# Row sums, block ends and embedding products of an attention layer at other places in TensorE's order

## The chip, the cores and the metric

The kernel runs on one core of a Trainium2 chip. Its engines work side by side, each through its own queue in order: TensorE (PE in the profile, its weight loads PEld), VectorE (DVE), ScalarE (ACT), GpSimd (POOL) and SyncE (SP), which here issues most of the DMA transfers. TensorE writes its results into PSUM banks; the others read them there. The metric is the device time of one execution in microseconds (us). The kernel before takes 2664.66 us, the median of three runs (2664.56 to 2665.32).

## The reference

Two layers on `x` of 2 x 512 x 64 x 32, so two images of 2048 tokens with 512 channels, all in float32. Only the first layer is touched by the change:

```python
q = concat(x, emb) @ Wq          # emb: 64 channels, made of row and column
k = concat(x, emb) @ Wk
v = x @ Wv
attn = softmax(q @ k.T / sqrt(64))        # 8 heads, 2048 x 2048 each
x = attn @ v @ Wout + bout + x
```

After it each token is normalized over its channels, and the second layer follows: a landmark attention with an iterated pseudo-inverse and a short convolution, and a feed-forward step whose two matrices the kernel multiplies into one (the "feed-forward map") while the first layer runs. The map is made of four-bit codes by compare and add on VectorE.

## The kernel before

The first layer is done as eight attentions, one for each image and pair of heads (two heads of 64 channels fill the 128 partitions): four of image 0, then four of image 1. `attention0` (L1263) does one of them. It has four query blocks `t` of 512 tokens, and for each 16 steps `c` of 128 keys: 64 steps, taken two at a time. One pass of its loop, two steps, is called a **round** here (round 0 to 31, and a last one, 32, without scores). A round does, in this order in the program:

- `scores` of its two steps: TensorE multiplies in the 64x64 form (L1275), ScalarE takes the exponential from PSUM to SBUF (L1283). There are two buffers for scores and six for exponentials.
- `add`: VectorE adds the exponentials into the running row sums of the block (L1293).
- `values` of the two steps of the round before: TensorE multiplies in the 64x64 form (L1305). At the last step of a block ScalarE copies one of the two result banks (L1311) and VectorE adds the other (L1312). There is one buffer for each of the two banks, so that the next block's first values wait for these two.
- a **burst**, where the round's number stands in `BURSTS`: a piece of other work on TensorE, mostly in the 128x128 form, taken from a generator up to its next `REST`.
- after a block's end the row sums: `sums_of` adds over the partitions with TensorE (L799), VectorE takes the reciprocal (L1320), eight transfers spread it (L810), GpSimd multiplies (L1323).
- in a round without a burst one call from the list `soon`, or, if that is empty and the round stands in `TABLE`, one step of the feed-forward map (L1359 to L1375).

The end of a block falls into rounds 8, 16 and 24, and that of the last block into round 32, before the next attention begins.

The bursts of an attention compute the next one's inputs (`Heads0.units`, L1065): for a pair of heads the embedding's part (`few`, L955, one small product for q and one for k, from which GpSimd or VectorE makes blocks `e`, L974), q and k in two halves (`products`, L1014, seven products each in a scheme of Strassen's kind, whose token differences VectorE makes at L911 by calls in `soon`), then the values (L1143), beside which steps of the feed-forward map run. Their end finds the largest |q| and |k| (L1126). The fifth attention's bursts also project, add and normalize image 0 (`finish0_units`: L1158 and L1165, then `statistics`, with a reciprocal at L1215). Banks of the projections, sums and normalization share two PSUM buffers (`bank`).

Each engine's order is the program's order; there is no planner. Lines below are the profile's.

Of the kernel before, what the change touches and what calls it, by code (L numbers as in the profile page):

```python
# [10 lines left out]
F32 = mybir.dt.float32  # L11
I32 = mybir.dt.int32
AF = mybir.ActivationFunctionType
# [3 lines left out]
P = 128  # L17
# [20 lines left out]
def general_path(  # L38
# [632 lines left out]
GAP = object()  # L671
REST = object()

TABLE = 9, 10, 11, 12, 16, 17, 18, 19, 20, 21, 22, 25, 27
NVS = 3, 3, 3, 1
FEW = (2, 1), (1, 2), (1, 1), (2, 2)
BURSTS = (
    *[(1, 6, 14, 23)] * 3, (4, 10, 17, 25), (1, 3, 6, 9, 11, 14, 17, 19, 22, 25, 27, 30),
    (4, 12, 21), (4, 12, 21), (12, 22),
)  # L680


# [1 line left out]
def fast_path(  # L684
# [99 lines left out]
    eps = const.tile([P, 1], F32, name="eps1")  # L784
    nc.vector.memset(eps, 1e-5)
    b0_sb = const.tile([P, KC], F32, name="b0_f")
    bound = const.tile([P, 3 * B * NPAIR], F32, name="bound1")
    zs = const.tile([P, 2], F32, name="zs1")
    rsum = const.tile([P, B * NPAIR, 4], F32, name="rsum1")
# [136 lines left out]
    class Heads0:  # L926
# [22 lines left out]
        def queries(self):  # L949
            self.q = qopool.tile([P, S], F32, tag="qo", name=f"q_{self.name}")  # L950

        def few(self, kind):

            fp = bank(f"fp_{kind}_{self.name}")
            nc.tensor.matmul(fp[:, : H + W], lhsT=self.w[kind][1], rhs=emb_sb, start=True, stop=True)  # L955
            ft = self.ft[kind] = wpool0.tile([P, H + W], F32, tag=f"ft{kind}", name=f"ft_{kind}_{self.name}")
            nc.vector.tensor_copy(ft, fp[:, : H + W])

        def embed(self, n=1):

# [105 lines left out]
        def units(self, xbs, parts, after=None, ready=None):  # L1066

            self.xbs = xbs
            self.begin()
            values = self.values()  # L1070
            if self.b == 0:
                for kind in "q" if self.plain else "qk":
                    self.few(kind)
                self.embed(4)
                yield
                yield REST
            if self.plain:
                for i, (kind, t) in enumerate(self.uses):
                    if i == 2 and self.b == 0:
                        self.few("k")  # L1080
                        self.embed(2)
                    if kind == "q" and self.b:
                        if t == 0:
                            yield from values
                            while not ready():
                                yield GAP
                    if kind == "q" and t == 0:
                        self.queries()
                    self.project(kind, t)
                    yield  # L1090
                if after:
                    after.begin()
            else:
                self.queries()
                if self.b and self.hp == 0:
                    for m in range(2):
                        next(values)
                        advance(ffn_map, 3)
                        yield
                    parts[0].begin()  # L1100
                    yield REST
                if not self.ws:
                    self.combine_w()
                    for _ in range(2):
                        next(values)
                        yield
                while ready and not ready():
                    yield GAP
                for tp in range(2):
                    yield from self.products(tp, parts[tp], parts[1] if tp == 0 else after)  # L1110
            if self.next:
                self.next.load()
                if self.next.b:
                    self.next.embed(4)
            for i, _ in enumerate(values):
                advance(ffn_map, NVS[i])
                yield
                if self.next and not self.next.plain and not self.next.ws:
                    self.next.combine_w()
            if self.next:  # L1120
                self.next.load("v")

            big = small.tile([P, 2], F32, tag="big0", name=f"big_{self.name}")

            def most(i, m):
                nc.vector.tensor_reduce(big[:, i : i + 1], m, AX.X, ALU.max, apply_absolute_value=True)  # L1126

            def both_of_them():
                most(1, self.k)
                i = self.b * NPAIR + self.hp  # L1130
                nc.vector.scalar_tensor_tensor(
                    bound[:, i : i + 1], big[:, :1], D**-0.5, big[:, 1:], ALU.mult, ALU.mult
                )

            most(0, self.q)
            soon.append(both_of_them)

    def values_of_tokens(v, t, xb, w_of, name):

# [30 lines left out]
    def deviation(name):  # L1170
        return apool.tile([P, TB], F32, tag="rstd", name=f"rstd_{name}", bufs=1)

    def statistics(xb, xn, part, name, squares, row, apart=False):
# [24 lines left out]
        nc.scalar.activation(rstd, var, AF.Sqrt, bias=eps, scale=1.0)  # L1198
        yield rstd

    def out0_units(b, t, xb, oTs):
# [4 lines left out]
    def norm0_steps(b, t, xb, xn, part, apart=False, halves=False):  # L1206

        toks = slice(t * TB, (t + 1) * TB)
        name = f"n0_{b}_{t}"
        squares = lambda: (xb[:, :2, :], xb[:, 2:, :])  # L1210
        for rstd in statistics(xb, xn, part, name, squares, lambda: deviation(name), apart):
            yield
        wide = rstd.unsqueeze(1).to_broadcast([P, 2, TB])

        nc.vector.reciprocal(rstd, rstd)  # L1215
        if halves:
            yield
        nc.gpsimd.tensor_tensor(xn[:, 2:, :], xn[:, 2:, :], wide, ALU.mult)
        nc.vector.tensor_tensor(xn[:, :2, :], xn[:, :2, :], wide, ALU.mult)
        nc.gpsimd.dma_start(chunked(xh_d[b])[:, :, toks], xn)  # L1220
        yield
# [38 lines left out]
                yield REST  # L1260
        yield from few(99)

    def attention0(hd, filler, needed, bursts, beside=None):  # L1263


        steps = [(t, c) for t in range(NTB) for c in range(NST)]
# [46 lines left out]
                late = t, its_acc  # L1313

        def sums(t, acc):
            o = hd.q[:, t * TB : (t + 1) * TB]
            rs = bank(f"rs_{hd.name}_{t}")
            sums_of(rs, acc)
            few = acc[:, 0, :LM]
            nc.vector.reciprocal(few, rs[:, :LM])  # L1320
            rinv = row_of(f"rinv_{hd.name}_{t}")
            spread(rinv, few)
            nc.gpsimd.tensor_tensor(o, o, rinv, ALU.mult)  # L1323

        pending = []
        for i in range(0, len(steps) + 1, GROUP):
            group = [(step, scores(*step)) for step in steps[i : i + GROUP]]
            for step, p in group:
                add(step, p)
            for step, p, its_acc in pending:  # L1330
                values(step, p, its_acc)
            pending = [(step, p, acc) for step, p in group]
            burst = i // GROUP in bursts
            if burst:
                advance(filler, len(steps), True)
            if not group:
                while needed in filler:
                    advance(filler)
            if late:
                sums(*late)  # L1340
                late = None
            if soon and not burst:
                soon.pop(0)()
            elif beside and not burst and i // GROUP in TABLE:
                advance(beside)

    def feed_forward_map():

# [678 lines left out]
    cur = heads[0]  # L2027
    cur.w = w0_first
    drain(units_of(0))
    oTs = []  # L2030
    for n, (b, hp) in enumerate(todo[:-1]):
        nb, nhp = todo[n + 1]
        if nb != b:
            xbs = load_x(x, nb, "x0")
        nxt = heads[n + 1]
        if n == NPAIR:
            outs_done = []
# [1 line left out]
            next(units)  # L2039
        else:  # L2040
            units = units_of(n + 1)
        attention0(cur, [units], units, BURSTS[n], ffn_map if n < NPAIR else None)
        oTs.append(cur.q)
        if n == 3:
            while ffn_map:
# [22 lines left out]
                yield REST  # L2068

    units = in_halves(pairs[0][0].keys_and_queries(qopool, "qo", xhs))  # L2070
    attention0(cur, [units], units, BURSTS[-1])
    oTs.append(cur.q)

    class Unit:
# [615 lines left out]
```

## Time and profile before

The profiled execution took 2662.55 us, with a span of 2660.7 us from its first to its last instruction; the granted TensorE clock was 0.999 of full speed. The table cuts the span at the first score of each attention.

| stretch, us | what | us | PE busy | DVE busy | ACT busy |
|---|---|---|---|---|---|
| 0 to 51.75 | loads, first q, k, v | 51.75 | 49.62 | 23.54 | 3.04 |
| 51.75 to 210.52 | attention 1 | 158.77 | 155.28 | 135.93 | 67.33 |
| 210.52 to 364.48 | attention 2 | 153.96 | 153.32 | 132.57 | 66.73 |
| 364.48 to 518.55 | attention 3 | 154.07 | 153.54 | 130.59 | 66.65 |
| 518.55 to 685.76 | attention 4 | 167.21 | 166.93 | 121.16 | 69.05 |
| 685.76 to 910.01 | attention 5 | 224.25 | 223.54 | 137.30 | 86.85 |
| 910.01 to 1062.77 | attention 6 | 152.76 | 152.48 | 123.79 | 66.74 |
| 1062.77 to 1215.53 | attention 7 | 152.76 | 152.48 | 107.46 | 66.73 |
| 1215.53 to 1360.00 | attention 8 | 144.47 | 144.18 | 98.86 | 69.19 |
| 1360.00 to 2660.70 | second layer | 1300.70 | 1281.14 | 759.70 | 345.36 |

A line of the page's groups reads: line, engine, operation, result and operands by the program's names, shapes, count; then busy us and mean ns of one; then the engine's idle us just before them and what ended it. A line of the timeline reads: start, duration, engine, line, operation, and in brackets the idle time before it with what released it. TensorE's matmuls overlap, so their durations are longer than the distance from one start to the next; the starts are the ruler. Each float32 matmul has two records.

### The profile page before, as it was taken

Reading aid. Unit: us, or ns where it says so; the run is one execution under the profiler, and the core shown is the slowest. Engines: PE = TensorE matmul, PEld = TensorE weight load, DVE = VectorE, ACT = ScalarE, POOL = GpSimd, SP = SyncE. Lnnn points to the kernel's source line nnn. Section 1 sums busy time; section 2 is a strip of 40 time slices with the busy share of each in tenths; the row PEclk is TensorE's granted clock in tenths of the full one; section 3 lists DMA queues with packets and bytes.
Section 4 is the critical chain, followed back from the end, with each engine's and each line's share of the span. In section 5 each row is a group of like instructions: output and inputs, shape, how many; then the busy total and the mean of one; then the engine's idle time right before and its main releaser. Section 6 shows DMA issues by size and latency. Waiting matters only on the chain.

```text
span 2660.7 us, 41330 instructions
## 1 busy us (share of the span) xinstructions
PE 2632.5 (99%) x16898; PEld 1345.3 (51%) x16898; DVE 1770.9 (67%) x2253; ACT 907.7 (34%) x1356; POOL 171.7 (6%) x127
## 2 busy tenths in 40 slices
PE   9999999999999999999999999999999999999998
PEld 5343433444344434343344455777677666665444
DVE  5798888986666677767668855545644646465665
ACT  1344344443343435345422323232323232231310
POOL 0102020000001100000002000000000000000000
PEclk9999999999999999999999999999999999999999
DMA  4001011201221220120115733313112112121211
GB/s 141 29 21 42 16 42 37 76 21 52 88 80 60 73 59 13 25 86 26 49 35 186 240 109 109 104 35 111 61 38 63 60 45 88 44 81 37 95 36 49
DMA packets 124759, 177.16 MB, mean 67 GB/s; under 512 B 16912, under 2 KB 78096, under 8 KB 122000
## 3 DMA queue, kind: packets, MB, share of 16 engines
q1 hardware_dynamic: 118416, 153.15, 18.2%
q0 software_dynamic: 5440, 20.97, 2.1%
q8 instruction: 134, 2.20, 0.4%
q14 instruction: 65, 0.53, 0.1%
q10 hardware_dynamic: 704, 0.31, 0.0%
HBM read 94.02 MB, written 63.57 MB: 59 GB/s over the span
## 4 chain that ended last, share of the span: by engine, by line
PE 93%; DVE 4%; ACT 1%; issue 1%; DMA 1%; SPq 0%; DVEq 0%; ACTq 0%
PE sc_f L1275 16%; PE av_f L1305 15%; PE pb L1827 5%; PE pa L1827 5%; PE vp_f L1143 4%; PE yp_g L1158 4%; PE fp_g L1983 4%; PE yp_f L1158 4%; PE vp L1143 4%; PE pc_f L1014 3%; PE pu L2093 3%; PE sc L1656 2%; PE pu_f L1014 2%; PE sc L1884 2%; PE av L1677 2%; PE pp L1478 2%
## 5 line engine op out<-in xcount | busy, mean ns | idle before, releaser
L1283 ACT ACTIVATE p_f<-sc_f 128x1024 f32<-128x1024 f32 x512 | 496.4, 1021 | 575.2 <-PE sc_f L1275 575.2
L1293 DVE TENSOR_TENSOR acc_f<-acc_f,p_f 128x1024 f32<-128x1024 f32 x448 | 576.4, 1287 | 149.1 <-ACT p_f L1283 120.9
L1275 PE MATMUL sc_f<-q_f,k_f 64*64 64x512 f32 x4096 | 489.9, 593 | 2.3 <-ACT p_f L1283 2.3
L1305 PE MATMUL av_f<-p_f,v_f 64*64 64x512 f32 x4096 | 486.7, 589 | 0.4 <-DVE q_f L1312 0.4
L1305 PEld LDWEIGHTS av_f<-p_f,v_f 64*64 64x64 f32 x4096 | 157.2, 133 | 285.3 <-issue 282.9
L1275 PEld LDWEIGHTS sc_f<-q_f,k_f 64*64 64x64 f32 x4096 | 148.3, 133 | 284.0 <-issue 263.1
L1827 PE MATMUL pa<-M 128*128 128x192 f32 (+1 forms) x640 | 150.3, 380 | 0.0
L1827 PE MATMUL pb<-R 128*128 128x192 f32 (+1 forms) x640 | 149.3, 380 | 0.3 <-DVE M L1840 0.3
L1323 POOL TENSOR_TENSOR q_f<-q_f,rinv_f 128x512 f32<-128x512 f32 x32 | 49.1, 1536 | 1128.4 <-DMA rinv_f<-acc_f 1028.6
L1143 PEld LDWEIGHTS vp_f<-wv_f,x 128*128 128x128 f32 x1024 | 115.6, 192 | 8.4 <-issue 8.4
L1827 PEld LDWEIGHTS pb<-R 128*128 128x128 f32 x640 | 106.6, 190 | 23.5 <-DVE M L1840 0.7
L1827 PEld LDWEIGHTS pa<-M 128*128 128x128 f32 x640 | 108.3, 193 | 19.8 <-ACT M L1818 2.0
L1143 PE MATMUL vp_f<-wv_f,x 128*128 128x128 f32 x1024 | 117.1, 276 | 0.0
L1158 PE MATMUL yp_g<-o,wo_f 128*128 128x512 f32 x256 | 113.8, 596 | 0.0
L1158 PE MATMUL yp_f<-q_f,wo_f 128*128 128x512 f32 x256 | 112.4, 594 | 0.0
L1143 PE MATMUL vp<-w,xh 128*128 128x128 f32 x896 | 105.9, 277 | 0.0
L1143 PEld LDWEIGHTS vp<-w,xh 128*128 128x128 f32 x896 | 102.1, 192 | 4.9 <-issue 3.0
L1840 DVE SCALAR_TENSOR_TENSOR M<-M,pb 128x320 f32<-128x320 f32 (+1 forms) x160 | 60.2, 418 | 60.7 <-PE pb L1827 60.7
L1983 PE MATMUL fp_g<-xn_g,mT 128*128 128x512 f32 (+1 forms) x232 | 99.3, 579 | 0.0
L1889 ACT ACTIVATE p<-sc 128x512 f32<-128x512 f32 x128 | 66.7, 602 | 91.3 <-PE sc L1884 90.8
L1921 POOL TENSOR_TENSOR o<-o,rinv 128x512 f32<-128x512 f32 x32 | 45.3, 1416 | 797.6 <-DVE rinv L1920 652.6
L1840 DVE SCALAR_TENSOR_TENSOR R<-M,pa 128x320 f32<-128x320 f32 (+1 forms) x160 | 58.5, 407 | 42.2 <-PE pa L1827 42.2
(278 smaller groups left out, 3197.7 us busy)
## 6 DMA issues: line engine op xcount, KB each, us to landing
xh<-xh_fd SPq DMA_DIRECT2D x12, 1024.0 KB, 5.8
rinv_f<-acc_f SPq DMA_DIRECT2D x256, 32.0 KB, 1.9
xr_f<-in_x_dram SPq DMA_DIRECT2D x8, 1024.0 KB, 5.1
x_fd<-xr_f POOLq DMA_DIRECT2D x8, 1024.0 KB, 4.7
xh_fd<-xn_f POOLq DMA_DIRECT2D x8, 1024.0 KB, 4.6
k<-k_fd SPq DMA_DIRECT2D x8, 1024.0 KB, 5.7
rinv<-acc SPq DMA_DIRECT2D x256, 32.0 KB, 1.8
x<-in_x_dram SPq DMA_DIRECT2D x7, 1024.0 KB, 5.6
```

The lines of the kernel that those rows point to most:

```text
L1014: nc.tensor.matmul(to, lhsT=w[:, k, :], rhs=x[:, k, :], start=start and k == 0, stop=k == 1, skip_group_check=True,)
L1143: nc.tensor.matmul(vp[:, j * P : (j + 1) * P], lhsT=xb[:, k, j * P : (j + 1) * P], rhs=w_of(k), start=k == 0, stop=k == KC - 1,)
L1158: nc.tensor.matmul(yp, lhsT=wo_sb[:, k, m * P : (m + 1) * P], rhs=oTs[k][:, toks], start=k == 0, stop=k == NPAIR - 1,)
L1275: nc.tensor.matmul(sc[r * D : (r + 1) * D, h, :], lhsT=hd.k[rows, lo : lo + D], rhs=hd.q[rows, t * TB : (t + 1) * TB], start=True, stop=True,)
L1283: nc.scalar.activation(p, sc, AF.Exp, scale=D**-0.5)
L1293: nc.vector.tensor_tensor(acc, first if c == 1 else acc, p, ALU.add)
L1305: nc.tensor.matmul(av[r][half, :], lhsT=hd.v[keys, c, half], rhs=pp[keys, h, :], start=c == 0, stop=c == NST - 1,)
L1827: nc.tensor.matmul(dst, lhsT=lhsT[:, k, t * P : (t + 1) * P], rhs=rhs[:, k, :], start=k == 0, stop=k == 1)
L1840: nc.vector.scalar_tensor_tensor(out, m, scale, pr, ALU.mult, ALU.subtract)
L1889: nc.scalar.activation(p[:, h, :], sc, AF.Exp, scale=D**-0.5)
L1983: nc.tensor.matmul(fp[:, cols], lhsT=mT[:, k, m * P : (m + 1) * P], rhs=self.xn[:, k, cols], start=k == 0, stop=k == KC - 1,)
L2093: nc.tensor.matmul(to, lhsT=w[:, k, :], rhs=x[:, k, :], start=start and k == 0, stop=k == 1, skip_group_check=True)
```

## The change

It moves work between places in the engines' orders; the matmuls stay the same.

- `TABLE` and `BURSTS` are new: most attentions have bursts at rounds 9, 17 and 25, just behind the block ends at 8, 16 and 24. Each of the first four attentions has its own list of rounds for the feed-forward map.
- A block's row sums wait for the next burst (or for a round with number 4 modulo 8) and are put at its front. ScalarE copies them out of PSUM, and VectorE takes the reciprocal behind the burst (`inverse`).
- The loop has no round 32. The last values of an attention and its sums are handed on as a function, which runs in round 0 of the next attention, between the first and the second group of scores.
- The embedding products of the next-but-one attention's head pair are made within the burst of values, in a buffer of the scores, and copied by ScalarE; the blocks `e` follow by a call in `soon`. The burst that held only them is gone.
- The first head pair's maxima are found before the first attention rather than in its rounds.
- Before the fourth attention four empty calls and the token differences of the second image go into `soon`; a `REST` after two units of values is gone.
- After each square root of the normalization in the fifth attention ScalarE takes one exponential, which loads that function's table again.

```diff
-TABLE = 9, 10, 11, 12, 16, 17, 18, 19, 20, 21, 22, 25, 27
+TABLE = *[(1, 2, 3, 4, 5, 6, 7, 22, 23, 28)] * 3, (13, 14, 18, 19, 20, 21, 22, 23, 24, 26, 27, 28), (), (), (), ()
+WAIT = 4
 BURSTS = (
-    *[(1, 6, 14, 23)] * 3, (4, 10, 17, 25), (1, 3, 6, 9, 11, 14, 17, 19, 22, 25, 27, 30),
-    (4, 12, 21), (4, 12, 21), (12, 22),
+    *[(9, 17, 25)] * 4, (2, 4, 7, 10, 12, 15, 18, 20, 23, 26, 28, 31),
+    (9, 17, 25), (9, 17, 25), (9, 17),
 )
...
-        def few(self, kind):
-            fp = bank(f"fp_{kind}_{self.name}")
-            nc.tensor.matmul(fp[:, : H + W], lhsT=self.w[kind][1], rhs=emb_sb, start=True, stop=True)
-            ft = self.ft[kind] = wpool0.tile([P, H + W], F32, tag=f"ft{kind}", name=f"ft_{kind}_{self.name}")
-            nc.vector.tensor_copy(ft, fp[:, : H + W])
+        def few(self, kinds, copy=nc.vector.tensor_copy):
+            fp = scores_bank(f"fp_{self.name}")
+            for kind, to in zip(kinds, (fp[:, 0, : H + W], fp[:, 1, : H + W])):
+                nc.tensor.matmul(to, lhsT=self.w[kind][1], rhs=emb_sb, start=True, stop=True)
+                ft = self.ft[kind] = wpool0.tile([P, H + W], F32, tag=f"ft{kind}", name=f"ft_{kind}_{self.name}")
+                copy(ft, to)
...
-            if self.b == 0:
-                for kind in "q" if self.plain else "qk":
-                    self.few(kind)
+            if self.b == 0 and self.plain:
+                self.few("q")
                 self.embed(4)
                 yield
-                yield REST
...
-                    parts[0].begin()
-                    yield REST
...
                 if self.next and not self.next.plain and not self.next.ws:
                     self.next.combine_w()
+                if self.next and self.next.b == 0 and i == 2:
+                    self.next.few("qk", nc.scalar.copy)
...
-            soon.append(both_of_them)
+            if self.plain and self.b == 0:
+                both_of_them()
+            else:
+                soon.append(both_of_them)
+            if self.next and self.next.b == 0:
+                soon.append(lambda: self.next.embed(4))
...
         nc.scalar.activation(rstd, var, AF.Sqrt, bias=eps, scale=1.0)
+        if back_to_exp:
+            nc.scalar.activation(table, eps, AF.Exp)
...
-            few = acc[:, 0, :LM]
-            nc.vector.reciprocal(few, rs[:, :LM])
+            nc.scalar.copy(acc[:, 0, :LM], rs[:, :LM])
+
+        def inverse(t, acc):
+            o, few = hd.q[:, t * TB : (t + 1) * TB], acc[:, 0, :LM]
+            nc.vector.reciprocal(few, few)
             rinv = row_of(f"rinv_{hd.name}_{t}")
             spread(rinv, few)
             nc.gpsimd.tensor_tensor(o, o, rinv, ALU.mult)
 
-        pending = []
-        for i in range(0, len(steps) + 1, GROUP):
+        def end():
+            for step, p, its_acc in pending:
+                values(step, p, its_acc)
+            sums(*late)
+            inverse(*late)
+
+        bursts, table, pending = BURSTS[n], TABLE[n], []
+        for i in range(0, len(steps), GROUP):
             group = [(step, scores(*step)) for step in steps[i : i + GROUP]]
             for step, p in group:
                 add(step, p)
+            if before:
+                before()
+                before = None
             for step, p, its_acc in pending:
                 values(step, p, its_acc)
             pending = [(step, p, acc) for step, p in group]
-            burst = i // GROUP in bursts
+            burst, summed = i // GROUP in bursts, None
+            if late and (burst or i // GROUP % 8 == 4):
+                summed, late = late, None
+                sums(*summed)
             if burst:
                 advance(filler, len(steps), True)
-            if not group:
-                while needed in filler:
-                    advance(filler)
-            if late:
-                sums(*late)
-                late = None
+            if summed:
+                inverse(*summed)
             if soon and not burst:
                 soon.pop(0)()
-            elif beside and not burst and i // GROUP in TABLE:
-                advance(beside)
+            elif not burst and i // GROUP in table:
+                advance(ffn_map)
+        while needed in filler:
+            advance(filler)
+        return end
...
         if nb != b:
             xbs = load_x(x, nb, "x0")
+            soon.extend([lambda: None] * WAIT)
+            parts_for(n + 1)[0].begin()
...
-        attention0(cur, [units], units, BURSTS[n], ffn_map if n < NPAIR else None)
+        end = attention0(cur, [units], units, n, end)
...
-    attention0(cur, [units], units, BURSTS[-1])
+    attention0(cur, [units], units, len(BURSTS) - 1, end)()
```

More of the change, by code (lines that the diff above doesn't have):

```diff
@@ L786, in fast_path @@
     b0_sb = const.tile([P, KC], F32, name="b0_f")
+    table = const.tile([P, 1], F32, name="table1")
     bound = const.tile([P, 3 * B * NPAIR], F32, name="bound1")
@@ L1171, in deviation, with statistics @@
         return apool.tile([P, TB], F32, tag="rstd", name=f"rstd_{name}", bufs=1)
-    def statistics(xb, xn, part, name, squares, row, apart=False):
+    def statistics(xb, xn, part, name, squares, row, apart=False, back_to_exp=False):
         nc.vector.tensor_tensor(part, xb[:, :2, :], xb[:, 2:, :], ALU.add)
@@ L1210, in norm0_steps @@
         squares = lambda: (xb[:, :2, :], xb[:, 2:, :])
-        for rstd in statistics(xb, xn, part, name, squares, lambda: deviation(name), apart):
+        for rstd in statistics(xb, xn, part, name, squares, lambda: deviation(name), apart, halves):
             yield
@@ L1261, in finish0_units, with attention0 @@
         yield from few(99)
-    def attention0(hd, filler, needed, bursts, beside=None):
+    def attention0(hd, filler, needed, n, before):
         steps = [(t, c) for t in range(NTB) for c in range(NST)]
@@ L1315, in sums @@
         def sums(t, acc):
-            o = hd.q[:, t * TB : (t + 1) * TB]
             rs = bank(f"rs_{hd.name}_{t}")
             sums_of(rs, acc)
-            few = acc[:, 0, :LM]
-            nc.vector.reciprocal(few, rs[:, :LM])
+            nc.scalar.copy(acc[:, 0, :LM], rs[:, :LM])
+        def inverse(t, acc):
+            o, few = hd.q[:, t * TB : (t + 1) * TB], acc[:, 0, :LM]
+            nc.vector.reciprocal(few, few)
             rinv = row_of(f"rinv_{hd.name}_{t}")
@@ L2029, in fast_path @@
     drain(units_of(0))
-    oTs = []
+    oTs, end = [], None
     for n, (b, hp) in enumerate(todo[:-1]):
```

## The prediction

> **What bounds the kernel now.** I read the page first, then the waits of TensorE, then the timeline around three places.
>
> ```profile
> span 2660.7 us, 41330 instructions
> PE 2632.5 (99%) x16898; PEld 1345.3 (51%) x16898; DVE 1770.9 (67%) x2253; ACT 907.7 (34%) x1356; POOL 171.7 (6%) x127
> ...
> PE 93%; DVE 4%; ACT 1%; issue 1%; DMA 1%; SPq 0%; DVEq 0%; ACTq 0%
> ...
> L1283 ACT ACTIVATE p_f<-sc_f 128x1024 f32<-128x1024 f32 x512 | 496.4, 1021 | 575.2 <-PE sc_f L1275 575.2
> L1293 DVE TENSOR_TENSOR acc_f<-acc_f,p_f 128x1024 f32<-128x1024 f32 x448 | 576.4, 1287 | 149.1 <-ACT p_f L1283 120.9
> L1275 PE MATMUL sc_f<-q_f,k_f 64*64 64x512 f32 x4096 | 489.9, 593 | 2.3 <-ACT p_f L1283 2.3
> L1305 PE MATMUL av_f<-p_f,v_f 64*64 64x512 f32 x4096 | 486.7, 589 | 0.4 <-DVE q_f L1312 0.4
> ```
>
> TensorE (PE) is the bound everywhere: 93% of the chain. The change adds no matmul and takes none away, so it can only win or lose what PE loses between matmuls: stalls, and switches between the 64x64 form of the attention and other forms. Matmul starts in the timeline give a tight ruler. A group (two steps) of scores, or of values, takes 1.717 us when the next is also 64x64; leaving 64x64 for another form adds 0.110 (1.827), returning adds 0.051 (1.768). A visit of the row sums costs 0.569 + 0.110 + 0.051 = 0.730.
>
> Start of an attention (here the second), with the sums that end the one before:
>
> ```profile
> 209.95 0.64 PE L799 MATMUL rs_f<-acc_f,ones 128*32 128x256 f32 x8 [0.23 <-DVE acc_f L1293]
> 210.52 1.95 PE L1275 MATMUL sc_f<-q_f,k_f 64*64 64x512 f32 x16
> 212.75 2.00 PE L1275 MATMUL sc_f<-q_f,k_f 64*64 64x512 f32 x16 [0.28 <-ACT p_f L1283]
> 214.58 1.90 PE L1305 MATMUL av_f<-p_f,v_f 64*64 64x512 f32 x16
> ```
>
> Two groups of scores run with no values between them. 210.52 to 214.58 is 4.06, where 2 x 1.717 + 0.051 = 3.49 would do: 0.57 lost to the exponentials.
>
> End of a query block (a boundary), in the first attention:
>
> ```profile
> 138.50 1.90 PE L1305 MATMUL av_f<-p_f,v_f 64*64 64x512 f32 x16
> 140.33 0.64 PE L799 MATMUL rs_f<-acc_f,ones 128*32 128x256 f32 x8
> 140.90 1.95 PE L1275 MATMUL sc_f<-q_f,k_f 64*64 64x512 f32 x16
> 141.05 0.69 DVE L1312 TENSOR_TENSOR q_f<-av_f,q_f 128x512 f32<-128x512 f32 x1
> 142.66 1.90 PE L1305 MATMUL av_f<-p_f,v_f 64*64 64x512 f32 x16
> ```
>
> VectorE (DVE) adds the block's two banks at 141.05 to 141.74; the next block's values, which need those banks, start at 142.66: 0.92 to spare, of which the sums' visit gives 0.73.
>
> The first products of the first attention:
>
> ```profile
> 82.25 2.99 PE L1014 MATMUL pc_f<-t,s_f 128*128 128x512 f32 x4 [2.98 <-DVE k_f L1029]
> 85.03 2.61 PE L1014 MATMUL pu_f<-t,s_f 128*128 128x512 f32 x4
> 87.48 1.88 PE L1014 MATMUL pc_f<-x,s_f 128*128 128x512 f32 x4
> ```
>
> PE stands 2.98 us for DVE, and the next matmuls are slow (2.99 and 2.61 against 1.88).
>
> **Gains, part by part.** (1) *First products.* This burst takes 17.16 us, the same one later 12.22: 4.94 lost. DVE was late because embedding sums, token differences and the 2.28 us maximum fell into the first five rounds. After the change the embedding products lie in the burst before, the maxima ahead of the attention, and the products in round 9 instead of 6. [...]the granted clock from 82 to 86 us is 0.64. I take 4.94.
>
> (2) *Attention starts.* The last values and sums go between the first two score groups. Before: 3.543 (32 values) + 0.569 + 4.056 = 8.168. After: 1.717 + 1.717 + 1.827 + 0.569 + 1.768 = 7.598. Seven starts x 0.57 = 4.0. The sums there waited for the adder 0.30, 0.42 and 0.03 in the first three: +0.75.
>
> (3) *Sums at the front of a burst.* Of four sums per attention three meet a burst (two in the last): 23. In the second layer sums are followed by a 128x128 form, and the step from the last of them to it is 0.31 us, as it is here to 64x64; so 0.569 stays, and one switch out and back, 0.161, is saved each time: 3.7.
>
> (4) *Four bursts fewer* (embedding bursts of three attentions, one in the fourth): 4 x 0.161 = 0.65. Their matmuls (0.61) only move.
>
> (5) *Other stalls.* One product burst in the third attention takes 12.73 for 12.22: 0.5, for DVE was late; with the sums ahead it has more time. In the fifth attention the bank addition stands behind the norm's reciprocal (3.35 us, 796.76 to 800.11) and PE loses 0.43 + 1.28 + 1.28 = 3.0 around it. With bursts at 7, 15, 23 that reciprocal falls after the addition. Gain of both 3.5.
>
> Gains: 4.94 + 4.75 + 3.7 + 0.65 + 3.5 = 17.5 us.
>
> **Losses.** ScalarE copies of the row sums: 32 x 0.37 = 12 us on an engine that waits 1.5 us in each 3.43 us round; nothing under that slack (without it a bank is held 0.4 longer each time, 12 in all). The early reload of the exponential's table, 1.28 x 4, moves within ScalarE, off PE's path (5 if it were on it). The six 96-column copies go to ScalarE in a burst where it has only four copies of 0.59 to do. Units of WAIT are empty. The reciprocal of merged sums and their eight transfers on SP (some 5 us to issue) come behind the burst's weight loads, so q is scaled a few rounds later; its next reader is over 50 us away, and the loads are ahead in the queue. The four transfers of an embedding come on SP in rounds 27 to 29, with nothing urgent behind them.
>
> What does cost: the sums leave the boundary, and with them 0.73 of 0.92. Each of the 21 boundaries outside the fifth attention keeps 0.19, less 0.06 from DVE's end to PE's start (801.78 to 801.84), so 0.13. If the values wait, the next scores stand behind them in PE's queue, and behind those the exponentials. DVE's queue decides. A plain round holds two additions, 2.66, in 3.43 us: it gains 0.77. A token difference makes it 3.60, 0.17 late per round; a step of the feed-forward map 3.53, 0.10 late. Now lay the queue after the burst at round 17: the reciprocal (1.75) stands behind the last evacuation and makes the first addition 0.95 late; four differences add 0.7; GpSimd's multiplication slows one operation by 1.07 (a difference of 1.22 takes 2.30 at 150.47); two map steps add 0.2. Sum 2.9 at round 24. The boundary's round has one addition fewer, which gives 1.33 back, and the margin 0.13: PE waits 1.4. That holds in attentions 1, 2 and 4: 4.3 us. In the third no differences follow: 0. In the sixth rounds 22 and 23 are plain and win 1.5 back: 0. At round 16 the two plain rounds cover it, save in the fourth attention, where a map step fills one: 0.5. At the start of the sixth attention reciprocal, normalization and maxima of the fifth (2.28 + 3.35 + 1.19 + 2.43), addition (0.69) and reciprocal (1.75) of its end come together, 11.7 against some 9.9 of slack until round 8: 1.8, and with GpSimd's share perhaps 2.8; less 1.33 and 0.13, 0.4 to 1.3: I take 1.3, as GpSimd did slow such work. At the other boundaries 0 to 0.1, taken at 0.05 x 16 = 0.8.
>
> The embedding sums now run on GpSimd in rounds 27 to 29 of the first two attentions, behind a 2.43 us maximum. [...] The row: from 60.11 to 67.12 four DVE operations of 1.22 took 1.79, 1.88, 2.07 and 2.07, 2.9 late. The closing sums bear 2.7 of lateness (they now stand 3.54 behind the values that the addition normally trails by 0.88). With maximum and burst before them 0.6 is left each by the row [...]: 1.2. In the fifth attention the reciprocal of the sums now stands ahead of the norm's first sums: 0.5.
>
> Losses: 4.3 + 0.5 + 1.3 + 0.8 + 1.2 + 0.5 = 8.6 us (bounds: 0 if DVE keeps up at every boundary, 17 at twice the lateness).
>
> **Sum.** 17.5 - 8.6 = 8.9 us off the profiled execution, whose own time is 2662.55 (span 2660.7 and 1.9 around it). The median is 2664.66, 2.1 more; the difference is carried over: **2655.8**.
>
> **Rivals.** (A) *DVE keeps up*: the lateness is not there and all 17.5 come, 2647. For it: until now only 2.4 us of weight-load waits are put down to that addition. Against: at burst 23 of the first attention DVE is 3.4 late already (the addition ends at 169.34; its exponential ended at 164.59, so 165.9 was possible), where nothing needs it. (B) *Half of the gain is returned*: lateness doubles, or burst 9 finds DVE as late as burst 6 did (4.94 back): 17.5 - 13 to 17, 2660 to 2664, no measurable change. For it: seven map steps in rounds 1 to 7 directly before a boundary. Against: 0.7 us in all, under the 1.33. (C) *Slower*: the bank addition becomes the bound at nearly every boundary: L1305 of each block's first values behind L1312, with 0.13 us to spare. Price: 24 boundaries x (lateness - 1.46). From a wait of 0.73 each it eats the 17.5; at the full 2.9 everywhere it is 35, or 2682. Against: most boundaries follow plain rounds. (D) *The move does not hide anything*: the values between the first scores stall for ScalarE as before; only 4.0 of the gain goes, 2659.8.
>
> **How the numbers follow.** A measurement of this kernel tells 0.2% (5.3 us) from no change. Forecast 0.50 (2651.5 to 2659.3), A 0.20, B 0.18, C 0.07, D 0.05 (split over the limit of 2659.3). Faster by over 0.2%: 0.50 + 0.20 + 0.02 + a share of B at its low edge 0.02 = 0.74; same 0.19; slower 0.07. The range leaves out C, the far half of B and the far end of A: 2647.5 to 2662.5.
>
> **What would show it.** The burst at about round 9 of the first attention at 12.2 us of products, clock 1.00; 16 scores, 16 values, 8 sums, 16 scores at each start; sums directly before L1014; fewer visits of L955. Waits of L1305 for L1312 of some 6 us in all, at round 24 of attentions 1, 2 and 4. It is wrong if those waits are spread over all boundaries (slower), or absent (A), or if the first products still wait for L1029.

## The result and the profile after

The kernel after takes 2656.73 us (median of 13 runs, 2655.94 to 2658.58); the kernel before, run between them on the same chip, 2663.6 (2660.8 to 2665.32). The ratio is 0.9976, with a 95% interval of 0.9968 to 0.9985: a gain of 0.24%, where 8.9 us or 0.33% was predicted. The profiled execution took 2656.73, 5.8 less than the profiled one before.

The page after, with the rows that answer to those of before (the lines have moved: L1275 is now L1285, L1283 is L1293, L1305 is L1315, L1312 is L1322, L799 is L801, L1014 is L1017):

```profile
span 2654.9 us, 41466 instructions
PE 2628.0 (99%) x16898; PEld 1352.7 (51%) x16898; DVE 1768.1 (67%) x2247; ACT 922.4 (35%) x1398; POOL 172.0 (6%) x127
...
PE 92%; DVE 6%; issue 1%; ACT 1%; DMA 1%; SPq 0%; DVEq 0%; ACTq 0%
...
L1293 ACT ACTIVATE p_f<-sc_f 128x1024 f32<-128x1024 f32 x512 | 496.7, 1022 | 539.2 <-PE sc_f L1285 539.1
L1303 DVE TENSOR_TENSOR acc_f<-acc_f,p_f 128x1024 f32<-128x1024 f32 x448 | 574.3, 1282 | 121.0 <-ACT p_f L1293 93.2
L1315 PE MATMUL av_f<-p_f,v_f 64*64 64x512 f32 x4096 | 490.3, 589 | 2.3 <-DVE q_f L1322 2.3
L1285 PE MATMUL sc_f<-q_f,k_f 64*64 64x512 f32 x4096 | 487.7, 591 | 0.3 <-ACT p_f L1293 0.3
```

The work is the same (16898 records of matmuls), and VectorE's share of the chain went from 4% to 6%. The two rows of matmuls show the exchange: the scores wait 0.3 us for the exponentials instead of 2.3, and the values 2.3 us for VectorE's bank addition (L1322) instead of 0.4. The page counts idle time from the modelled ends of the matmuls, so it shows less of these waits than the starts do, which are summed below.

The first products, in round 9 (timeline of TensorE):

```profile
84.55 1.90 PE L1315 MATMUL av_f<-p_f,v_f 64*64 64x512 f32 x16
86.37 0.64 PE L801 MATMUL rs_f<-acc_f,ones 128*32 128x256 f32 x8
86.94 1.98 PE L1017 MATMUL pc_f<-x,wk_f 128*128 128x512 f32 x4
88.76 1.88 PE L1017 MATMUL pu_f<-x,wk_f 128*128 128x512 f32 x4
90.48 1.88 PE L1017 MATMUL pc_f<-t,s_f 128*128 128x512 f32 x4
```

Nothing waits; from 86.94 to 99.16 the burst takes 12.22, as predicted, and the sums stand directly before it. The start of the second attention:

```profile
206.48 1.90 PE L1285 MATMUL sc_f<-q_f,k_f 64*64 64x512 f32 x16
208.20 1.90 PE L1315 MATMUL av_f<-p_f,v_f 64*64 64x512 f32 x16
210.52 0.64 PE L801 MATMUL rs_f<-acc_f,ones 128*32 128x256 f32 x8 [0.42 <-DVE acc_f L1303]
211.09 1.95 PE L1285 MATMUL sc_f<-q_f,k_f 64*64 64x512 f32 x16
212.85 1.90 PE L1315 MATMUL av_f<-p_f,v_f 64*64 64x512 f32 x16
```

The order is the one drawn in the prediction, and the second scores no longer wait for the exponentials. The sums wait for the adder: their visit comes 2.32 after the values, not 1.83.

The boundary at round 24 of the first attention, TensorE first and then VectorE:

```profile
161.93 1.90 PE L1315 MATMUL av_f<-p_f,v_f 64*64 64x512 f32 x16
163.65 1.90 PE L1285 MATMUL sc_f<-q_f,k_f 64*64 64x512 f32 x16
165.37 1.03 PE L1315 MATMUL av_f<-p_f,v_f 64*64 64x512 f32 x4
167.44 1.93 PE L1315 MATMUL av_f<-p_f,v_f 64*64 64x512 f32 x12 [1.04 <-DVE q_f L1322]
169.31 0.64 PE L801 MATMUL rs_f<-acc_f,ones 128*32 128x256 f32 x8
```

```profile
164.50 0.42 DVE L1393 TENSOR_SCALAR hits_f<-tmp_f 128x512 f32<-128x512 f32 x1
164.96 0.69 DVE L1394 TENSOR_TENSOR wl_f<-wl_f,hits_f 128x512 f32<-128x512 f32 x1
165.57 1.22 DVE L1303 TENSOR_TENSOR acc_f<-p_f,p_f 128x1024 f32<-128x1024 f32 x1
166.71 0.68 DVE L1322 TENSOR_TENSOR q_f<-av_f,q_f 128x512 f32<-128x512 f32 x1
```

Four records (two matmuls) of the new block's values run into the first bank, and the rest stand until the second bank is added. The addition starts 4.78 after the block's last values (166.71 - 161.93); at the boundary shown before it was 2.55 (141.05 - 138.50). That is 2.23 later. Without the sums' visit 0.73 of the 0.92 to spare is gone, so the wait should be 2.23 - 0.19 = 2.04; the starts give 2.11 (169.31 - 165.37 = 3.94, where 1.827 would do).

The embedding pair, now within the burst of values:

```profile
180.79 0.46 PE L958 MATMUL fp_f<-emb_f,weq_f 64*128 64x96 f32 x2
181.38 0.24 ACT L960 COPY ft_q_f<-fp_f 128x96 f32<-128x96 f32 x1
181.68 0.46 PE L958 MATMUL fp_f<-emb_f,wek_f 64*128 64x96 f32 x2 [0.43 <-ACT ft_q_f L960]
182.06 3.84 PE L1149 MATMUL vp_f<-wv_f,x 128*128 128x128 f32 x32
```

The product for k waits until ScalarE has copied the one for q, though it goes to the other bank of the buffer. A pair takes 1.27 us (180.79 to 182.06). The kernel before had a buffer for each product, and a pair took 0.62 us there (216.40 to 217.02):

```profile
216.40 0.46 PE L955 MATMUL fp_q_f<-emb_f,weq_f 64*128 64x96 f32 x2
216.70 0.38 PE L955 MATMUL fp_k_f<-emb_f,wek_f 64*128 64x96 f32 x2
217.02 1.95 PE L1275 MATMUL sc_f<-q_f,k_f 64*64 64x512 f32 x16
```

Summed over all matmul starts of the first layer (up to the first out-projection of the second image: 1357.07 us before, 1351.00 after):

| part | before, us | after, us | gain |
|---|---|---|---|
| bursts of products | 151.93 | 146.37 | 5.55 |
| loss at scores (starts, and returns to 64x64: 55 before, 28 after) | 8.12 | 2.76 | 5.36 |
| leaving 64x64, the switch alone (69 and 42 times 0.110) | 7.59 | 4.62 | 2.97 |
| leaving 64x64, waits | 3.75 | 9.14 | -5.39 |
| embedding products, and the bursts of values around them | 119.14 | 121.18 | -2.04 |
| plain products of q and k (ahead of the first attention, in the fifth and in the eighth) | 84.20 | 84.62 | -0.42 |

These come to 6.0 of the 6.07. The 9.14 of waits are 7.3 for the bank addition, at seven boundaries (2.11, 1.75 and 1.68 at round 24 of attentions 1, 2 and 4; 0.43 at round 16 of the fourth, 0.89 at round 8 of the sixth, 0.22 and 0.21 at two more), and 1.84 for the closing sums, those at an attention's end (0.49, 0.96 and, at the very end, 0.39). The second layer took 0.3 more than before.

### The profile page after: what moved, and what is told of

It is laid out like the page before. It is cut to its first block, busy times and chain, and to the rows that moved or that the text cites. A ratio compares the mean times of both kernels' runs of the same rounds, so it can differ in the third digit from the quotient of the medians.

```text
span 2654.9 us, 41466 instructions
## 1 busy us (share of the span) xinstructions
PE 2628.0 (99%) x16898; PEld 1352.7 (51%) x16898; DVE 1768.1 (67%) x2247; ACT 922.4 (35%) x1398; POOL 172.0 (6%) x127
## 4 chain that ended last, share of the span: by engine, by line
PE 92%; DVE 6%; issue 1%; ACT 1%; DMA 1%; SPq 0%; DVEq 0%; ACTq 0%
PE sc_f L1285 15%; PE av_f L1315 15%; PE pb L1850 5%; PE pa L1850 5%; PE vp_f L1149 4%; PE yp_g L1164 4%; PE fp_g L2006 4%; PE yp_f L1164 4%; PE vp L1149 4%; PE pc_f L1017 3%; DVE acc_f L1303 3%; PE pu L2118 3%; PE pu_f L1017 2%; PE sc L1679 2%; PE sc L1907 2%; PE av L1700 2%
## 5 line engine op out<-in xcount | busy, mean ns | idle before, releaser
L1293 ACT ACTIVATE p_f<-sc_f 128x1024 f32<-128x1024 f32 x512 | 496.7, 1022 | 539.2 <-PE sc_f L1285 539.1
L1315 PE MATMUL av_f<-p_f,v_f 64*64 64x512 f32 x4096 | 490.3, 589 | 2.3 <-DVE q_f L1322 2.3
L1285 PE MATMUL sc_f<-q_f,k_f 64*64 64x512 f32 x4096 | 487.7, 591 | 0.3 <-ACT p_f L1293 0.3
L1315 PEld LDWEIGHTS av_f<-p_f,v_f 64*64 64x64 f32 x4096 | 160.5, 133 | 286.2 <-issue 277.2
L1285 PEld LDWEIGHTS sc_f<-q_f,k_f 64*64 64x64 f32 x4096 | 152.3, 133 | 283.7 <-issue 280.1
```

Of the source, the lines that this page charges most:

```text
L1285: nc.tensor.matmul(sc[r * D : (r + 1) * D, h, :], lhsT=hd.k[rows, lo : lo + D], rhs=hd.q[rows, t * TB : (t + 1) * TB], start=True, stop=True,)
L1293: nc.scalar.activation(p, sc, AF.Exp, scale=D**-0.5)
L1315: nc.tensor.matmul(av[r][half, :], lhsT=hd.v[keys, c, half], rhs=pp[keys, h, :], start=c == 0, stop=c == NST - 1,)
```

## The experiments

Theory: the bank waits are VectorE's lateness, built up by token differences, map steps and the reciprocal behind the burst, with a threshold at the boundary; and the pair of embedding products holds itself up. Rivals: the waits come from taking the sums away from the boundary, whatever VectorE does; ScalarE's copies, not VectorE, hold the banks; or the gain at the first products is due to the new form of the code and not to the rounds. The runs with one profiled execution are read by their matmul starts, since single times of one kernel differ by up to 2.6 us (after) or 4.5 us (before).

**The pair without its own wait.** Both products are issued before either copy.

```diff
-            for kind, to in zip(kinds, (fp[:, 0, : H + W], fp[:, 1, : H + W])):
+            made = [(kind, fp[:, i, : H + W]) for i, kind in enumerate(kinds)]
+            for kind, to in made:
                 nc.tensor.matmul(to, lhsT=self.w[kind][1], rhs=emb_sb, start=True, stop=True)
+            for kind, to in made:
                 ft = self.ft[kind] = wpool0.tile([P, H + W], F32, tag=f"ft{kind}", name=f"ft_{kind}_{self.name}")
                 copy(ft, to)
```

> The changed kernel, with both embedding products issued before both copies. In the changed kernel the four records of a pair take 1.27 us where they took 0.61, since the second product waits for the copy of the first. If the copy standing between the two matmuls is the cause, each pair falls back to 0.61: 3 x 0.66 = 2.0 us less, a span of 2652.9 instead of 2654.9. If the scores' buffer itself is slow to come free, nothing changes: 2654.9.

Measured 2655.34 us, span 2653.5. In the timeline the pair now stands close:

```profile
180.24 0.46 PE L959 MATMUL fp_f<-emb_f,weq_f 64*128 64x96 f32 x2
180.54 0.38 PE L959 MATMUL fp_f<-emb_f,wek_f 64*128 64x96 f32 x2
180.86 3.39 PE L1151 MATMUL vp_f<-wv_f,x 128*128 128x128 f32 x28
```

180.24 to 180.86 is 0.62. The embedding products fell from 4.60 to 2.61, 1.99 as expected; the layer gained 1.63, for the first closing sums waited 0.83 instead of 0.49 and the first q products, which the edit does not touch, took 0.33 more (the second closing sums and the start of the program took 0.3 less). The 2.0 us were the order of two matmuls and two copies in one buffer. In the kernel after, the second product's weight load waits 0.59 us for ScalarE's copy (the copy ends at 181.62, the load starts at 181.67), which stands ahead of it in the program; in this run the product stands ahead of that copy.

**Plain rounds before the boundaries.** Map steps leave rounds 22, 23 and 28 (in the fourth attention 22 and 23) and stand in the boundaries' own rounds.

```diff
-TABLE = *[(1, 2, 3, 4, 5, 6, 7, 22, 23, 28)] * 3, (13, 14, 18, 19, 20, 21, 22, 23, 24, 26, 27, 28), (), (), (), ()
+TABLE = *[(1, 2, 3, 4, 5, 6, 7, 8, 16, 24)] * 3, (8, 13, 14, 16, 18, 19, 20, 21, 24, 26, 27, 28), (), (), (), ()
```

> The changed kernel, with the map steps of rounds 22, 23 and 28 put into rounds 8, 16 and 24 (fourth attention: 22 and 23 into 8 and 16), so that rounds 22 and 23 are plain ones. Lateness theory: two plain rounds take 2 x 0.87 off VectorE's lateness at round 24; the waits there go from 2.11, 1.75 and 1.69 to 0.4, 0 and 0, and the closing sums' waits from 0.49 and 0.96 to 0 and 0.1: 6.4 less, span 2648.5. If the waits come from the missing sums alone, whatever VectorE's lateness, they stay: 2654.9. If work directly before a burst only shifts the wait to the burst's first products, less than half comes: above 2652.

Measured 2651.47 us, span 2649.6. The same boundary:

```profile
161.98 1.90 PE L1315 MATMUL av_f<-p_f,v_f 64*64 64x512 f32 x16
163.70 1.90 PE L1285 MATMUL sc_f<-q_f,k_f 64*64 64x512 f32 x16
165.42 1.90 PE L1315 MATMUL av_f<-p_f,v_f 64*64 64x512 f32 x16
167.24 0.64 PE L801 MATMUL rs_f<-acc_f,ones 128*32 128x256 f32 x8
```

The wait of 2.11 is gone, as are 1.75, 0.22, 0.21 and the closings' 0.49 and 0.96; 1.68 became 0.13. Left are 0.44 (fourth attention, round 16), 0.89 (sixth, where no map step stood) and 0.39. The first layer gained 7.23, the same sums still being away from the boundary: the rival that blames their absence alone falls, and so does the embedding sums' part in the closings, since GpSimd adds at the same place here (193.22 to 201.20 us in the first attention, 193.62 to 201.67 in the kernel after). What decided there is the map steps of rounds 22, 23 and 28, which were moved together; the share of each was not tried. The second layer took 1.9 us more, 1.5 of it in matmuls at half the clock; see the last section.

**ScalarE copies both banks.** VectorE then adds from SBUF, and its lateness holds no bank.

```diff
                 nc.scalar.copy(o, av[0])
-                nc.vector.tensor_tensor(o, av[1], o, ALU.add)
+                other = row_of(f"other_{hd.name}_{t}")
+                nc.scalar.copy(other, av[1])
+                nc.vector.tensor_tensor(o, other, o, ALU.add)
```

> The changed kernel, with the second bank of a block's values copied out by ScalarE as the first is, and VectorE adding from SBUF later, so that the banks do not wait for VectorE. If VectorE's queue is what the next block's values wait for, all 7.3 us of those waits go (the second copy ends some 1.3 us after the values, the next ones start 1.72 after), the closing sums' 1.8 stay: span 2647.6. If ScalarE becomes late in its place (two copies of 0.59 in a row, the exponentials behind them), half or less comes: 2651 or more.

Measured 2651.78 us, span 2650.0. ScalarE and VectorE at the same boundary:

```profile
163.86 0.59 ACT L1321 COPY q_f<-av_f 128x512 f32<-128x512 f32 x1 [0.60 <-PE av_f L1315]
...
164.34 0.59 ACT L1323 COPY other_f<-av_f 128x512 f32<-128x512 f32 x1
...
165.36 1.90 PE L1315 MATMUL av_f<-p_f,v_f 64*64 64x512 f32 x16
...
166.34 0.69 DVE L1324 TENSOR_TENSOR q_f<-other_f,q_f 128x512 f32<-128x512 f32 x1
```

The addition is still late (166.34, after the new values began), and nothing waits for it. All seven bank waits are gone; the closing sums' are not (0.93, 1.02, 0.39), since those need the adder itself. The layer gained 6.79, and 7.3 were expected: the closing sums wait 0.5 longer. The span is 2.4 over the 2647.6 expected, as the second layer took 1.8 more (last section). So VectorE's place in the chain, not ScalarE's, made the waits, and the second copy of 0.59 us on ScalarE costs nothing visible.

**The reciprocal at the front of the burst,** with the sums, instead of behind its evacuations.

```diff
                 sums(*summed)
+                inverse(*summed)
             if burst:
                 advance(filler, len(steps), True)
-            if summed:
-                inverse(*summed)
```

> The changed kernel, with the reciprocal and its transfers ahead of the burst instead of behind it. If VectorE's lateness at round 24 is made of the terms that the prediction added up (0.95 of the reciprocal and 1.07 of GpSimd's multiplication after the burst), both are now spent inside the burst: the waits of 2.11, 1.75, 1.68 and 0.43 go to 0.1 or 0, the closing sums' 0.49 and 0.96 shrink too: 6 to 7 us less, span 2648 to 2649. If the burst's first products then wait for their evacuation behind the reciprocal, up to 0.5 in each of 14 bursts comes back: 2655.

Measured 2651.06 us, span 2649.2; the layer gained 5.42, under the 6 to 7 expected. The waits fell from 9.14 to 1.71 (0.20, 0.83 and 0.39 at boundaries and end, and 0.29 in the fifth attention), so the reciprocal's place was as needful to the lateness as the map steps: taking either away brings it under the threshold. The expectation's second case, a burst that waits behind the reciprocal, came in one place (waits of TensorE):

```profile
PE yp_f L1164 <- DVE xr_f L1171: 1.1, 3, 0.4
```

In the fifth attention's bursts the out-projection has two buffers, and the reciprocal now stands ahead of the VectorE operation that frees them: the bursts of its out-projection went from 55.72 to 57.62. The bursts of products stayed at 146.38 (146.37 in the kernel after). The place behind the burst is right in the fifth attention, and wrong in the others.

**Sums at the boundary again,** the reciprocal still behind the next burst.

```diff
-        bursts, table, pending = BURSTS[n], TABLE[n], []
+        bursts, table, pending, summed = BURSTS[n], TABLE[n], [], None
...
-            burst, summed = i // GROUP in bursts, None
-            if late and (burst or i // GROUP % 8 == 4):
+            burst = i // GROUP in bursts
+            if late:
                 summed, late = late, None
                 sums(*summed)
...
-            if summed:
+            if summed and (burst or i // GROUP % 8 == 4):
                 inverse(*summed)
+                summed = None
```

> The changed kernel, with the row sums back at the block's end in rounds 8, 16, 24 (their reciprocal stays behind the burst). By the prediction's steps two effects cancel: 23 more switches out and back at 0.161 cost 3.7, and the 0.73 between the values takes 0.73 (or the whole) off each boundary wait, 7.3 to 3.5: net -0.1, span 2654.8 (2654.3 to 2655.3). If the waits have nothing to do with the sums' place, the switches alone show: 2658.6. If the move of the sums is what the change gains, it is slower by 3 or more.

Measured 2657.52 us, span 2655.7: the layer is 0.51 longer than in the kernel after, where 0.1 shorter was expected. There are 23 more visits, 3.7 us of switches, and the waits fall by 3.1, to 6.03. Most of them change their kind:

```profile
PE rs_f L801 <- DVE acc_f L1303: 4.0, 7, 0.8
```

It is the sums that wait for VectorE's adder now (4.5 us by the starts, at seven places); the values still wait 0.50 for the bank at round 24 of attentions 1, 2 and 4. So moving the sums to the bursts, step (3), won its 3.7 and gave back nearly all of it, because VectorE was late at just those boundaries; it pays only where VectorE is in time.

**Rounds alone.** The kernel before, with the first attention's bursts at later rounds.

```diff
-    *[(1, 6, 14, 23)] * 3, (4, 10, 17, 25), (1, 3, 6, 9, 11, 14, 17, 19, 22, 25, 27, 30),
+    (1, 9, 17, 25), *[(1, 6, 14, 23)] * 2, (4, 10, 17, 25), (1, 3, 6, 9, 11, 14, 17, 19, 22, 25, 27, 30),
```

> The kernel before, with the product bursts of its first attention in rounds 9, 17 and 25 instead of 6, 14 and 23; all else (embedding burst in round 1, maxima, sums at the block's end) as it was. If the first products wait because VectorE is late in round 6 and the three rounds more let it catch up, the 4.9 us there go: span 2655.8 instead of 2660.7, clock 1.00 throughout the first attention. If the embedding products had to come earlier for that, the wait stays: 2660.7, or half of it.

Measured 2664.48 us, span 2662.6, where 2655.8 was expected. The products' wait goes (151.93 to 146.97) with the rounds alone, without any other part of the change. But VectorE's queue held its work somewhere:

```profile
82.37 1.90 PE L1305 MATMUL av_f<-p_f,v_f 64*64 64x512 f32 x16
86.06 0.64 PE L799 MATMUL rs_f<-acc_f,ones 128*32 128x256 f32 x8 [1.79 <-DVE acc_f L1293]
86.62 1.95 PE L1275 MATMUL sc_f<-q_f,k_f 64*64 64x512 f32 x16
```

The sums of the first block wait 1.86 for the adder, behind the same differences and the maximum. The fifth attention's first out-projection stands 0.9 us for weights that arrive late, the bursts of its out-projection grow from 55.72 to 57.91, and the first q and k took 1.6 more: in sum the layer is 1.1 longer than before. The kernel after has no such wait: its maxima are found before the first attention.

**The hand-on alone.** The kernel before, with an attention's last values and sums put behind the next one's first scores (the function `end` and the call of `before` as in the change).

```diff
+            if before:
+                before()
+                before = None
             for step, p, its_acc in pending:
                 values(step, p, its_acc)
```

> The kernel before, with nothing but the hand-on of an attention's last values and sums to round 0 of the next. By the prediction's step: 7 starts x 0.57 and the closing sums' waits of 0.75, 4.7 less, span 2656.0. If the values between the first scores still stall for ScalarE, 1 to 2 us less at most: 2659 or more.

Measured 2662.28 us, span 2660.5; the layer gained 2.11, where 4.7 was expected. The starts' 0.57 are gone, all but the first, and so are the closing sums' 0.75: 4.7, as expected. The rest is not the edit's doing, or was not foreseen. The product bursts took 1.7 less, since this execution had no halved clock there (1.00 from 78 to 86 us; last section). Against that stand 1.7 in the program's first 53 us, which the edit does not touch, and new waits of 2.6 at the start of the sixth attention (timelines of TensorE and of VectorE):

```profile
910.47 1.03 PE L1305 MATMUL av_f<-p_f,v_f 64*64 64x512 f32 x4
913.06 1.50 PE L1305 MATMUL av_f<-p_f,v_f 64*64 64x512 f32 x10 [1.56 <-DVE q_f L1312]
```

```profile
905.79 3.35 DVE L1215 RECIPROCAL rstd_n<-rstd_n 128x512 f32<-128x512 f32 x1
909.05 2.23 DVE L1126 TENSOR_REDUCE big_f<-q_f 128x1 f32<-128x2048 f32 x1
911.20 1.21 DVE L1293 TENSOR_TENSOR acc_f<-p_f,p_f 128x1024 f32<-128x1024 f32 x1
912.32 0.68 DVE L1312 TENSOR_TENSOR q_f<-av_f,q_f 128x512 f32<-128x512 f32 x1
```

The norm's reciprocal and the maximum stand ahead of the bank addition, and the values at 910.47 follow the sums by 2.34 us (908.13), where before two groups of scores and the exponentials lay between. The prediction feared this pile of work and put it at round 8; there the kernel after has its 0.89.

**The three remedies together,** the pair, the plain rounds and the two copies, on the kernel after.

> The changed kernel with the pair of embedding products ahead of their copies, the map steps in rounds 8, 16 and 24, and ScalarE copying both banks. Their separate gains in the first layer were 1.6, 7.2 and 6.8; the last two remove the same waits, and only 0.44 + 0.13 + 0.89 are left to the third: 1.6 + 7.2 + 1.5 = 10.3, a span of 2644.6 (1.7 more if the clock is halved for a window in the second layer), so a ratio of about 0.9935 to the kernel before. If the gains exclude each other, 2647 or more.

Measured 2647.16 us (median of 5, 2645.68 to 2648.11), against 2662.82 of the kernel before: ratio 0.9938, 0.9924 to 0.9951. The layer gained 10.63, where 10.3 was expected; of the waits only 0.57 (first start) and 0.56 (the end) remain. Its chain:

```profile
PE 96%; DVE 2%; ACT 0%; SPq 0%; issue 0%; DMA 0%; DVEq 0%; ACTq 0%
```

VectorE is at 2%, where the kernel after has 6. This version beats both kernels: the interval of its ratio lies below the kernel after's (0.9968 to 0.9985).

## Why the prediction was nearly right

The time was 2656.73 for 2655.8, inside the range; in one profiled execution against the other, 5.8 gained for 8.9. That the time came within 0.9 us is in part luck. Between the medians the gain was 6.9, so 2.0 of the 8.9 did not come; but the median that the forecast was taken from was 1.1 above that of the thirteen runs, and the gain that was set too high fell on nearly the right time. By its own steps:

- **(1) First products, right.** The burst takes 12.22. But the term is not one number. In the profiled run before, 3.2 were the wait and 1.7 the clock: the kernel with the hand-on alone had the same wait, 2.97 us for L1029, with a granted clock of 1.00 in 82 to 86 us, and its product bursts summed to 150.20 instead of 151.93. Taking the whole 4.94 priced that one execution rightly, and this other one by 1.7 too much. In which of the thirteen runs of the kernel before the clock was halved there is not on record.
- **(2) Starts, right.** Loss at scores fell by 5.36, where 7 x 0.57 + 27 x 0.051 = 5.37 was due. The 0.75 of closing waits went too, and others came (below).
- **(3) and (4), the switches, right:** 27 fewer exits, 2.97 us.
- **(4) "Their matmuls (0.61) only move", wrong.** This is the step that failed: a term put at nothing. The two products share a buffer, and the second is issued behind ScalarE's copy of the first; each pair takes 1.27. Three pairs are 1.98; the cuts in the bursts of values cost 0.49, and the first two products, at the program's start, gained 0.43. That is 2.04, the largest part of the missing 3.1. The diff showed it: the copy stands inside the loop over the two kinds. The copies were costed on ScalarE, and it was not asked who waits for them.
- **(5) Other stalls, right:** the fifth attention's 0.43 + 1.28 + 1.28 are gone, and the third's 0.5 (products 5.55 for 5.44).
- **Boundaries, right in mechanism and in place, some too small.** 5.54 at round 24 of attentions 1, 2 and 4 (predicted 4.3), 0.43 in the fourth at round 16 (0.5), 0.89 in the sixth (1.3), 0.43 at the others (0.8): 7.3 for 6.9. Of the lateness, 2.23 was left after the boundary's own relief, for the 2.9 - 1.33 = 1.57 of the prediction.
- **Closing sums, the size and the reason off:** 1.84 for 1.2, of which 0.39 at the very end was not foreseen. GpSimd's embedding sums were blamed alone; moving the map steps away removed 0.49 and 0.96 with those sums in place.
- **What was costed at nothing** and cost nothing visible: the copies of the row sums, the table reloads, the transfers on SP. The fifth attention's 0.5 was at most 0.16 (one group of q products, 7.14 for 6.99). The plain products of q and k took 0.42 more with that group, the rest ahead of the first attention (among the other runs of the kernel after's kind they lie from 0.8 under to 0.3 over it), and the second layer 0.3.

Together: -2.04 - 0.4 - 0.6 - 0.4 - 0.3, with 0.5 and 0.1 the other way, is -3.1.

Rival A, that VectorE keeps up, is refuted by seven bank waits; but its number, 17.5 us, was there to be had: the change and the three remedies together gain 6.07 + 10.63 = 16.7 in the first layer, 1.7 of it the clock. C, waits at nearly every boundary, is refuted by 14 boundaries of 21 without one; its mechanism is real, at a third of them. D is refuted at every start. B did not come: round 9 found VectorE in time.

## What to carry to other kernels

When a change takes work off the bound engine's path at a hand-over, ask what that work was hiding: here a visit of 0.73 us covered another engine's lateness, and moving it gave its gain back (3.7 won, 3.1 returned) until that lateness was cut or the buffer freed by an idle engine. Lateness acted by a threshold here, so that one remedy of several suffices, and two together don't add up (7.2 and 6.8 alone, 10.6 with a third worth 2.0). And for each instruction that is moved, look not only at the engine it lands on, but at who is issued behind it into the same buffer.

## What the hardware showed

The clock halved for a stretch of 3.41 us in one execution, and not in another with a wait as long. In the kernel before it did so from 83.08 to 86.50 us, 0.83 us after the wait of 2.98 had ended: the granted clock was 0.64 from 82 to 86 us, and TensorE had been busy for 0.83 us of the 3.41 before the stretch. With the hand-on alone the wait was 2.97, and the granted clock was 1.00 from 78 to 86 us.

Near 2475 us, in the second layer, TensorE waits for ScalarE a few times (0.18 us and 0.79 us with plain rounds); in that kernel the next feed-forward products ran slow (a row of the timeline, then the stretch from 2474 to 2478 us: its length, the busy time and instructions of the five engines, the granted clock, 0.57, the DMA share and GB/s):

```profile
2474.95 8.63 PE L2006 MATMUL fp_g<-xn_g,mT 128*128 128x512 f32 x16
```

```profile
2474.00:2478.00 4.00, 4.00 (x6) 1.54 (x6) 2.20 (x4) 1.27 (x3) 1.01 (x1) 0.57 0.09 25
```

The same row takes 7.13 in the kernel after, so this stretch costs 1.5. Three more runs had a slower stretch near there, each over two slices of 4 us: two copies (0.70 from 2474 us and 0.87 from 2478), hand-on alone (0.94 from 2482 and 0.63 from 2486), and all three (0.62 from 2470 and 0.96 from 2474). By these clocks each would be about 3.4 us at half and cost up to 1.7, an estimate. From 2466 to 2490 us the kernel before and the kernel after were at 1.00.

Idle time alone doesn't tell where it happens. In the kernel after TensorE stood at the same two products (L1907) for 0.19 and 0.79 us before that row, idle for 0.97 us from 2478 to 2482 as with plain rounds from 2470 to 2474, and the clock stayed at 1.00. What decides was not shown.
